# Attention over active tokens: values of later batches from the score stacks, and context products kept together

## The chip, the cores and the metric

The kernel runs on one core of one Trainium2 chip. The metric is device time in microseconds (us). The core has TensorE (PE, matrix products into PSUM), VectorE (DVE), ScalarE (ACT), GpSimd (POOL) and SyncE (SP), each with its own queue, worked off in order. TensorE's weight loads are listed apart, as PEld. DMA transfers are issued from SyncE's queue and, for rows picked by an index, from GpSimd's.

## The reference

There are 16 batches; x is 16 x 512 x 1024 (features x tokens). The queries serve as keys and as values too.

```python
xt = transpose(x, (0, 2, 1))                         # tokens x 512
q = xt @ Wq.T;  qh = q in 8 heads of 64
scores = 0.125 * einsum('bhqd,bhkd->bhqk', qh, qh)
logits = (scores * cmask + (1 - cmask) * -1e30) * rmask
ctx = einsum('bhqk,bhkd->bhqd', softmax(logits), qh)
x = x + transpose(ctx @ Wo.T)
```

The mask is 0 or 1 for each token. A masked key gets no weight. For a masked query all logits are equal, and its context is the mean of q over all tokens.

## The kernel before, in words

**Tokens.** Of each batch only the active tokens, at most C = 544, go through attention. An index is built on the chip from the mask (`active`, `slots`, `hot`, `index`), and `gather` fetches rows of x by it: four blocks of 128 slots and a tail of 32 (CT). Inactive tokens only get the projected mean added (`rest`).

**Stages of a batch n.** `xt` transposes a block on TensorE and splits it into two float16 parts, xh and xl. `query(n, e, g)` makes q for a pair of heads e (128 features) and half g of the slots, in 12 products. `qsplit(n, e)` then splits q of the pair into hi and lo float16 parts (`hl`), and four DMAs of SyncE spread them into the *score stack* xx. Its slices 0 and 2 hold, for the two heads of the pair, hi in partitions 0 to 63 and lo in partitions 64 to 127; slices 1 and 3 hold the same with hi and lo exchanged. The DMAs are not issued at once: `later` puts them off to the next step. There are five buffers for stacks, and a batch has four.

`value(n, e)` (L484) turns q of a pair into values, slots in the partitions, by four float32 transposes (L489), copies them to `v` on ScalarE (L491) and sums their squares for the softmax's shift (`peaks`, `top`, `bottom`: the largest norm of a head bounds its scores; group 0 is heads 0 to 3, group 1 heads 4 to 7). Six buffers hold `v`. `value_tail` does the same for the tail slots.

`scores(b, p, i)` makes four products of the stack (L611, 128 keys x 544 queries in two halves), and ScalarE takes their exponential (L615) into a tile of p. `scores(b, p, None)` does the tail keys of four heads (L586). `attend(b, p, i)` adds the context of one block of keys for a pair of heads to `pav`: four float32 products, two halves by two heads (L629). Each of them appears as two matmuls in the profile, "passes" below. Block 4 is the tail (L632). `recip_sums` and `recip_rows` make the reciprocals of the sums, `norm` multiplies them in, and `project` multiplies by Wo (L712) and adds to x; rows leave by an indirect DMA. `project_means` projects the means of a group of batches.

**What sets the order.** `run` goes through the batches. Batch b has 18 steps: for four pairs of heads p the blocks i = 0 to 3, and two tail steps. A step makes the scores of one head, then works off a share of a list m of other work, then makes the scores of the second head. The list m holds the projection of batch b - 1, the second shift group of b, and the transposes, queries, values and first shift group of batch n = b + 1, each item with a cost in us; `fill` takes from it in proportion. The contexts of two steps are put off and then called together, as a *context group*:

```python
if i in (0, 2):
    ready, todo = todo, []
elif i in (1, 3):
    for f in ready[1::-1] + ready[2:]:
        f()
    ready = []
```

Two attends make 8 float32 products, 16 passes. The order in which the instructions come to stand in an engine's queue is then settled by the framework's scheduler, which weighs priorities and its own estimates of when an operand is ready; so other work may come between two products of a group. `behind(i)` keeps what is recorded under it after instruction i, and `high_priority` lets it go ahead of other work that is ready.

Tiles of PSUM: two buffers for scores, one for `pav`, two (`pm`) for everything else.

Of the kernel before, what the change touches and what calls it, by code (L numbers as in the profile page):

```python
# [12 lines left out]
F16 = mybir.dt.float16  # L13
I32 = mybir.dt.int32
AF = mybir.ActivationFunctionType
ALU = mybir.AluOpType
# [3 lines left out]
P = 128  # L20
# [3 lines left out]
DK = 64  # L24
# [8 lines left out]
CH = C // 2  # L33
# [13 lines left out]
HPO = 300  # L47


class Fast:  # L50
# [12 lines left out]
    def __init__(self, ctx, tc, x, x_nat, mask_t, wq_t, wo_t, out):  # L63
        self.tc, self.nc = tc, tc.nc
        self.x, self.x_nat, self.out = x, x_nat, out
        self.B = x.shape[0] // T
        pool = lambda name, bufs, **k: ctx.enter_context(tc.tile_pool(name=name, bufs=bufs, **k))
        self.const = pool("const", 1)
        self.one = pool("one", 1)
        self.dram = pool("dram", 8, space=bass.MemoryType.DRAM)  # L70
        self.ps_s = pool("ps_s", 2, space=PS)
        self.ps_av = pool("ps_av", 1, space=PS)
        self.ps_m = pool("ps_m", 2, space=PS)
        self.st = {}
        self.scatters = []
        self.exp, self.pool = [], []

        self.paced, self.beat = False, None
        self.urgent, self.spare = [], []

        self.soon = []
        self.w, self.raw = {}, {}
        self.src = {"q": wq_t, "o": wo_t}
        self.setup(mask_t)
# [44 lines left out]
    def setup2(self):  # L129
        nc, fixed = self.nc, self.fixed  # L130

        self.quad = fixed("quad", [P, HG])
        nc.vector.tensor_reduce(self.quad, self.ident.rearrange("p (r t) -> p r t", r=HG), AX.X, ALU.add)
        self.xh = fixed("xh", [P, DC, CQ], F16)
        self.xl = fixed("xl", [P, DC, CQ], F16)
        for t in (self.xh, self.xl):
            nc.gpsimd.memset(t[:, :, CM + 1:], 0.0)

        self.rcol = [fixed("rcol%d" % k, [P, P]) for k in range(2)]
        self.smcol = [fixed("smcol%d" % k, [P, P]) for k in range(2)]  # L140
        for t in self.rcol + self.smcol:
            nc.gpsimd.memset(t, 0.0)

        self.big = fixed("big", [P, self.B + 2 * DC])

        self.par = fixed("par", [P, 2])
        nc.vector.tensor_tensor(self.par, self.quad[:, 0:2], self.quad[:, 2:4], ALU.add)
# [335 lines left out]
    def value(self, b, e):  # L483
        nc, s = self.nc, self.st[b]  # L484
        if e == 0:
            s["sd"] = self.sb([P, DC, H], F32, "sd")
        pv = self.pm([P, 4, P])
        for k in range(4):
            nc.tensor.transpose(pv[:, k, :], s["q"][:, e, k * P:(k + 1) * P], self.ident)  # L489
        v = self.sb([P, 4, P], F32, "v", 6)  # L490
        nc.scalar.copy(v, pv)  # L491
        s["v"].append(v)
        self.squares(v.rearrange("p k (h d) -> p (k h) d", h=2), s["sd"][:, e, :], e < 2 if b == 0 else e == 0, b == 0)
# [126 lines left out]
    def attend(self, b, p, i, ps):  # L620
        nc, s = self.nc, self.st[b]

        if i == 1:
            s["pav"] = self.ps_av.tile([P, 2, 512], F32, tag="av", name="pav")
        for g in range(2):
            for k in (1, 0) if i < 4 else range(2):
                cols = slice(g * CH, (g + 1) * CH)
                if i < 4:
                    nc.tensor.matmul(s["pav"][k * DK:(k + 1) * DK, g, :CH], lhsT=s["v"][p][:, i, k * DK:(k + 1) * DK],  # L629
                                     rhs=ps[k][:, cols], start=(i == 1), stop=False)  # L630
                else:
                    nc.tensor.matmul(s["pav"][:, g, :CH], lhsT=s["vt"][p // 2][:, k, p % 2 * 2:p % 2 * 2 + 2, :],  # L632
                                     rhs=s["pt"][:, p % 2, cols], start=False, stop=(k == 1))
        if i == 4:
            c = self.sb([P, C], F32, "c", 4)
            nc.scalar.copy(c.rearrange("p (g c) -> p g c", g=2), s["pav"][:, :, :CH])
            s["c"].append(c)
# [192 lines left out]
    def run(self, flag):  # L830
        B = self.B
        L = lambda f, *a: lambda: f(*a)
# [5 lines left out]
        def xt(n):  # L838
            return [(0.45, L(self.xt, n, c)) for c in range(4)] + [(0.25, L(self.xt, n, 4))]

        def query(n, e, g):
            u = [(1.37, L(self.query, n, e, g))]
            return u + [(0, L(self.qsplit, n, e))] if g else u

        def value(n, e):
            return [(0.45, L(self.value, n, e))]
# [8 lines left out]
        for i, e in enumerate(ends):  # L855
            g = list(range(ends[i - 1] + 1 if i else 0, e + 1))
# [73 lines left out]
        if True:  # L930
            for b in range(B + 1):
                o, n = b - 1, b + 1
# [3 lines left out]
                free, sums, rows, third, tail, rest = {}, [], [], [], [], []  # L936
                if b:
                    sums, rows, third = [(0, L(self.recip_sums, o, 3))], [(0.1, L(self.recip_rows, o, 3))], [(0, L(self.norm, o, 3))]
                if n < B:
                    if b in tails:  # L940
                        free[0] = [L(self.late, o, 4)]
                        tail = [(2.6, L(self.project_tail, o))]
# [3 lines left out]
                second = [(0, L(self.norm, o, 2))] if b else []  # L946
                P_ = (lambda *i: project(o, *i)) if b else (lambda *i: [])
                pk, tp, bt = ((lambda o, g, f=f, c=c: [(c, L(f, o, g))]) for f, c in ((self.peaks, 0), (self.top, 0.1), (self.bottom, 0.1)))
                new = [g for g in groups if b == g[0] - 2], [g for g in groups if b == g[0] - 1]
                if n < B:  # L950
                    q, x, v = (lambda e, g: query(n, e, g)), xt(n)[2 if b == 0 else 0:], (lambda e: value(n, e))
                    tc, tv = ((lambda g, f=f, c=c: [(c, L(f, n, g))]) for f, c in ((self.tail_copy, 0), (self.value_tail, 0.25)))
                    rng = [(0, L(self.range_x, n, c)) for c in range(DC)]
                    ahead = b + 2 < B
                    hot, index = ([(c, L(f, b + 2))] if ahead else [] for f, c in ((self.hot, 0), (self.index, 0.2)))
                    take = [(0, L(self.gather, b + 2, j)) for j in range(5)] if ahead else []
                    m = sums + pk(b, 1) + x[:2] + second + x[2:4] + rows + x[4:]
                    for g in new[0]:
                        m += [(0, L(self.active, *g))]
                    m += q(0, 0) + tp(b, 1) + q(0, 1)  # L960
                    for g in new[0]:
                        m += [(0.3, L(self.slots, *g))]
                    for g in new[1]:
                        m += [(0, L(self.facts_sums, *g))]
                    m += bt(b, 1) + q(1, 0) + v(0) + third + q(1, 1)
                    for g in new[1]:
                        m += [(0.1, L(self.facts_end, *g))]
                    m += tc(0) + rng[:2] + tail + v(1) + P_(0) + tv(0) + rest + P_(1) + hot + rng[2:] + q(2, 0) + index
                    m += pk(n, 0) + q(2, 1) + tp(n, 0) + P_(2) + take + v(2) + q(3, 0) + bt(n, 0)
                    m += q(3, 1) + tc(1) + [(0, L(self.means, n))] + P_(3) + v(3) + tv(1)  # L970
                    if b == 0:
                        k = next(k for k, (c, f) in enumerate(m) if f is index[0][1])
                        for c in range(DC):
                            m.insert(k + 1 + 3 * c, (0, L(self.split, "o", c)))
                else:

                    places = [("xi", 8), ("xa", 13)]
                    come = [[L(self.late, x, j, *places[k % 2]) for j in range(5, 9)] for k, x in enumerate(rests[b])]
                    leave = [[L(self.rest, x, j) for j in range(5, 9)] for x in rests[b]]
                    free[0] = [L(self.late, b, 4)] + come[0]  # L980
                    for c, l in zip(come[1:] + [[]], leave):
                        free[0] += c + l
                    m = second + sums + pk(b, 1) + [(2.6, L(self.project_means, b))] + rows + [(0.6, lambda: None)]
                    m += tp(b, 1) + [(0.6, lambda: None)] + bt(b, 1) + [(1.2, lambda: None)] + third + [(1.2, lambda: None)] + P_(0, 1, 2, 3)
                if b == 1:
                    m += [(0, L(self.range_w, "o", c)) for c in range(DC)]
                if b == B - 1:
# [1 line left out]
                if b == 0:  # L989
                    m = begin + m  # L990
# [22 lines left out]
                for st, (p, i) in enumerate(S):  # L1013
# [16 lines left out]
                    if i in (0, 2):  # L1030
                        ready, todo = todo, []
                    elif i in (1, 3):
                        for f in ready[1::-1] + ready[2:]:
                            f()
                        ready = []
# [158 lines left out]
```

## Time and profile before

| | |
|---|---|
| median of 3 runs | 1074.26 us (1073.34 to 1080.06) |
| profiled execution | 1082.2 us, span 1080.5 us |
| TensorE busy | 1053.5 us, 98% of the span |
| VectorE, ScalarE, GpSimd busy | 739.3, 679.0, 317.5 us |
| TensorE clock granted | 0.993 of full speed over the span |

In the page's groups a row names the line, the engine, the operation, the tiles written and read, their shapes and the count; then come busy time and the mean length of one in ns, and after the second bar the engine's idle time just before these instructions, with what ended most of it. Matmuls overlap: [...]the next starts long before it ends. In the timeline a line is a run of equal instructions: start, length, engine, line and count. The difference of two starts is what a run takes of TensorE's time. The lines quoted are of line numbers before the change; in the changed kernel 489 becomes 497, 629 becomes 643 and 586 becomes 595.

### The profile page before, as it was taken

Reading aid. Unit: us, or ns where it says so; the run is one execution under the profiler, and the core shown is the slowest. Engines: PE = TensorE matmul, PEld = TensorE weight load, DVE = VectorE, ACT = ScalarE, POOL = GpSimd, SP = SyncE. Lnnn points to the kernel's source line nnn. Section 1 sums busy time; section 2 is a strip of 40 time slices with the busy share of each in tenths; the row PEclk is TensorE's granted clock in tenths of the full one; section 3 lists DMA queues with packets and bytes.
Section 4 is the critical chain, followed back from the end, with each engine's and each line's share of the span. In section 5 each row is a group of like instructions: output and inputs, shape, how many; then the busy total and the mean of one; then the engine's idle time right before and its main releaser. Section 6 shows DMA issues by size and latency. Waiting matters only on the chain.

```text
span 1080.5 us, 23254 instructions
## 1 busy us (share of the span) xinstructions
PE 1053.5 (98%) x8386; PEld 698.3 (65%) x8386; DVE 739.3 (68%) x2375; ACT 679.0 (63%) x1722; POOL 317.5 (29%) x303
## 2 busy tenths in 40 slices
PE   7899999999999999999999999999999999999996
PEld 6566666666666666666666666666666676666553
DVE  5698668676765767767685676958577676757553
ACT  4786667566666756657666666766667565655550
POOL 2101022232401222332322323223232322234643
PEclk8999999999999999999999999999999999999999
DMA  5756565546655654666556566554765555466652
GB/s 186 218 152 167 138 175 157 170 139 191 173 141 156 170 168 145 189 192 172 175 143 194 168 182 188 154 172 134 211 190 171 179 149 154 134 179 195 193 165 85
DMA packets 78122, 181.35 MB, mean 168 GB/s; under 512 B 15008, under 2 KB 16800, under 8 KB 78000
## 3 DMA queue, kind: packets, MB, share of 16 engines
q1 hardware_dynamic: 56816, 111.62, 37.1%
q0 software_dynamic: 21184, 68.18, 19.8%
q8 instruction: 68, 1.11, 0.4%
q14 instruction: 54, 0.44, 0.1%
HBM read 92.34 MB, written 33.91 MB: 117 GB/s over the span
## 4 chain that ended last, share of the span: by engine, by line
PE 88%; DVE 5%; ACT 3%; issue 2%; DMA 1%; POOL 0%; another core or an unknown queue 0%; POOLq 0%; SPq 0%; ACTq 0%; DVEq 0%
PE pav L629 23%; PE pss L611 21%; PE pm L443 15%; PE pm L712 14%; PE pm L420 3%; PE pav L632 3%; PE pm L489 2%; PE pss L586 2%; PE pm L665 1%; ACT p L615 1%; PE pm L511 1%; ACT xm L365 1%; PE warm L303 1%; ACT p L590 1%; DVE p L596 1%
## 5 line engine op out<-in xcount | busy, mean ns | idle before, releaser
L615 ACT ACTIVATE p<-pss,nm 128x544 f32<-128x544 f32 x512 | 365.9, 717 | 231.8 <-PE pss L611 221.8
L611 PE MATMUL pss<-xx 128*128 128x272 f16 x2048 | 314.1, 280 | 3.2 <-ACT p L615 2.3
L629 PE MATMUL pav<-p,v 128*64 128x272 f32 x2048 | 273.5, 401 | 0.0
L611 PEld LDWEIGHTS <-xx 128*128 128x128 f16 x2048 | 193.1, 100 | 77.8 <-issue 31.3
L629 PEld LDWEIGHTS pav<-p,v 128*64 128x64 f32 x2048 | 131.9, 136 | 94.4 <-issue 34.0
L796 POOL DMA_INDIRECT y_out<-xa,idx x68 | 68.7, 1011 | 283.2 <-PE pss L611 83.9
L443 PE MATMUL pm<-xh,wqh 128*128 128x274 f16 (+1 forms) x512 | 143.7, 281 | 3.1 <-DVE xa L717 2.2
L443 PE MATMUL pm<-xh,wql 128*128 128x274 f16 (+1 forms) x512 | 143.2, 280 | 0.0
L443 PE MATMUL pm<-xl,wqh 128*128 128x274 f16 (+1 forms) x512 | 143.1, 280 | 0.0
L335 POOL DMA_INDIRECT xa<-x_in,idx x68 | 76.4, 1124 | 174.6 <-PE pss L611 64.4
L443 PEld LDWEIGHTS <-wqh 128*128 128x128 f16 x1024 | 99.1, 99 | 26.0 <-issue 7.1
L796 POOL DMA_INDIRECT y_out<-xi,idx x60 | 76.8, 1280 | 121.9 <-PE pss L611 43.3
L615 ACT ACTIVATION_READ_ACCUMULATOR p<-pss,nm 128x1 f32 x512 | 103.5, 202 | 0.0
L717 DVE SCALAR_TENSOR_TENSOR xa<-pm,xa 128x512 f32<-128x512 f32 x60 | 41.4, 690 | 87.7 <-PE pm L712 83.6
L335 POOL DMA_INDIRECT xi<-x_in,idx x60 | 62.1, 1036 | 109.8 <-PE pss L611 39.0
L712 PE MATMUL pm<-woh,ch 128*128 128x512 f16 x240 | 91.1, 379 | 0.0
L712 PE MATMUL pm<-woh,cl 128*128 128x512 f16 x240 | 91.0, 379 | 0.0
L712 PE MATMUL pm<-wol,ch 128*128 128x512 f16 x240 | 91.0, 379 | 0.0
L446 ACT ACTIVATE q<-pm 128x272 f32<-128x272 f32 (+1 forms) x128 | 50.6, 395 | 60.0 <-PE pm L443 52.5
L712 PEld LDWEIGHTS <-ch 128*128 128x128 f16 x480 | 46.4, 98 | 45.7 <-issue 1.3
L365 ACT ACTIVATE xm<-xm 128x1024 f32<-128x1024 f32 (+1 forms) x62 | 62.5, 1009 | 1.9 <-DMA xm<-x_nat_in 1.9
L783 DVE TENSOR_TENSOR xi<-xi,ub 128x512 f32<-128x512 f32 (+1 forms) x60 | 41.3, 691 | 30.5 <-PE pss L611 28.5
(191 smaller groups left out, 1562.5 us busy)
## 6 DMA issues: line engine op xcount, KB each, us to landing
xx<-hl SPq DMA_DIRECT2D x256, 136.0 KB
xm<-x_nat_in SPq DMA_DIRECT2D x56, 512.0 KB
rb<-rd SPq DMA_DIRECT2D x128, 136.0 KB
pt<-c SPq DMA_DIRECT2D x64, 136.0 KB
pt<-p SPq DMA_DIRECT2D x64, 136.0 KB
ub<-ud SPq DMA_DIRECT2D x16, 256.0 KB
xi<-x_nat_in SPq DMA_DIRECT2D x8, 256.0 KB
xa<-x_in,idx POOLq DMA_INDIRECT x68
```

What stands on the lines that cost most here:

```text
L335: dma = self.nc.gpsimd.indirect_dma_start(out=tile[:n], out_offset=None, in_=self.x, in_offset=bass.IndirectOffsetOnAxis(ap=idx, axis=0))
L365: self.nc.scalar.activation(s["xm"][k], s["xm"][k], AF.Copy, accum_out=s["ms2"][:, k:k + 1])
L420: self.pe = nc.tensor.transpose(pt[:, c, :], x[:n, c * P:(c + 1) * P], self.ident[:n, :n]).ins
L443: self.beat = nc.tensor.matmul(pq, lhsT=w[:, c, e * P:(e + 1) * P], rhs=xx[:, c, cols], start=(k == 0), stop=(k == 3 * DC - 1)).ins
L446: nc.scalar.activation(s["q"][:, e, cols], pq, AF.Copy, scale=1.0 / (SX * SW))
L611: self.beat = nc.tensor.matmul(pt[:, g, :CH], lhsT=xx[:, 2 * k, i * P:(i + 1) * P], rhs=xx[:, 2 * k + a, g * CH:(g + 1) * CH], start=(a == ...
L615: self.exp = [nc.scalar.activation(t.rearrange("p (g c) -> p g c", g=2), pt[:, :, :CH], AF.Exp, bias=s["nm"][p // HG][:, p % HG:p % HG + 1 ...
L629: nc.tensor.matmul(s["pav"][k * DK:(k + 1) * DK, g, :CH], lhsT=s["v"][p][:, i, k * DK:(k + 1) * DK], rhs=ps[k][:, cols], start=(i == 1), s ...
L712: nc.tensor.matmul(po[:cols.stop - cols.start], lhsT=a[:, e, cols], rhs=w[:, e, :], start=(e == 0 and k == 0), stop=(e == DC - 1 and k == 2))
L717: self.nc.vector.scalar_tensor_tensor(x, po, 1.0 / (SX * SW), x, ALU.mult, ALU.add)
L783: self.once(self.nc.vector.tensor_tensor(x[:n], x[:n], s["ub"][:n], ALU.add), self.beat)
L796: dma = self.nc.gpsimd.indirect_dma_start(out=self.out, out_offset=bass.IndirectOffsetOnAxis(ap=idx, axis=0), in_=x, in_offset=None)
```

## The change

Values of batches 1 to 15 are made of the score stack. A slice of it, 128 slots wide, is the stationary operand, and the moving one is `two`, a 128 x 64 float16 tile made of two identities one above the other. The product adds hi and lo of a head and puts slots into the partitions. A pair of heads takes 4 blocks x 2 heads = 8 products, in place of 4 transposes. Batch 0 keeps the transposes.

```diff
+        self.two = fixed("two", [P, DK], F16)
+        nc.vector.tensor_tensor(self.two, self.ident[:, :DK], self.ident[:, DK:], ALU.add)
...
         for k in range(4):
-            nc.tensor.transpose(pv[:, k, :], s["q"][:, e, k * P:(k + 1) * P], self.ident)
+            if b == 0:
+                nc.tensor.transpose(pv[:, k, :], s["q"][:, e, k * P:(k + 1) * P], self.ident)
+            else:
+                for h in range(2):
+                    nc.tensor.matmul(pv[:, k, h * DK:(h + 1) * DK], lhsT=s["xx"][e][:, 2 * h, k * P:(k + 1) * P],
+                                     rhs=self.two, start=True, stop=True)
```

The first product of a context group is remembered, and the group's others are recorded behind it with a high priority. `run` clears the memory ahead of each group.

```diff
                 if i < 4:
-                    nc.tensor.matmul(s["pav"][k * DK:(k + 1) * DK, g, :CH], lhsT=s["v"][p][:, i, k * DK:(k + 1) * DK],
-                                     rhs=ps[k][:, cols], start=(i == 1), stop=False)
+                    with ExitStack() as st:
+                        if self.group_first:
+
+                            st.enter_context(self.behind(self.group_first))
+                            st.enter_context(self.tc.high_priority(offset=HPO))
+                        mm = nc.tensor.matmul(s["pav"][k * DK:(k + 1) * DK, g, :CH], lhsT=s["v"][p][:, i, k * DK:(k + 1) * DK],
+                                              rhs=ps[k][:, cols], start=(i == 1), stop=False)
+                    self.group_first = self.group_first or mm.ins
...
                     elif i in (1, 3):
+                        self.group_first = None
```

A value now needs the stack's transfers, so the list m is put in another order. Values 0 to 2 of batch n stand further behind their queries. Value 3 goes into the next batch's list, ahead of the peaks of shift group 1. In batch 0 the index of batch 2 and its gathers come earlier. In the last batch the product of means comes later.

```diff
-                    m = sums + pk(b, 1) + x[:2] + second + x[2:4] + rows + x[4:]
+                    m = sums + x[:2] + (value(b, 3) if b else []) + pk(b, 1) + second + x[2:4] + rows + x[4:]
...
-                    m += q(0, 0) + tp(b, 1) + q(0, 1)
+                    m += q(0, 0) + tp(b, 1) + (q(0, 1) if b else bt(b, 1) + q(0, 1))
...
-                    m += bt(b, 1) + q(1, 0) + v(0) + third + q(1, 1)
+                    m += (bt(b, 1) if b else hot) + q(1, 0) + third + ([] if b else index) + q(1, 1) + ([] if b else take)
...
-                    m += tc(0) + rng[:2] + tail + v(1) + P_(0) + tv(0) + rest + P_(1) + hot + rng[2:] + q(2, 0) + index
-                    m += pk(n, 0) + q(2, 1) + tp(n, 0) + P_(2) + take + v(2) + q(3, 0) + bt(n, 0)
-                    m += q(3, 1) + tc(1) + [(0, L(self.means, n))] + P_(3) + v(3) + tv(1)
+                    m += rng[:2] + tc(0) + tail + v(0) + P_(0) + tv(0) + rest + v(1) + P_(1) + (hot if b else []) + rng[2:] + q(2, 0) + (index if b else [])
+                    m += pk(n, 0) + q(2, 1) + tp(n, 0) + P_(2) + (take if b else []) + q(3, 0) + v(2) + bt(n, 0)
+                    m += q(3, 1) + tc(1) + [(0, L(self.means, n))] + P_(3) + tv(1)
...
-                    m = second + sums + pk(b, 1) + [(2.6, L(self.project_means, b))] + rows + [(0.6, lambda: None)]
-                    m += tp(b, 1) + [(0.6, lambda: None)] + bt(b, 1) + [(1.2, lambda: None)] + third + [(1.2, lambda: None)] + P_(0, 1, 2, 3)
+                    m = second + sums + value(b, 3) + pk(b, 1) + rows + [(0.6, lambda: None)]
+                    m += tp(b, 1) + [(0.6, lambda: None)] + bt(b, 1) + [(2.6, L(self.project_means, b))] + third + [(1.2, lambda: None)] + P_(0, 1, 2, 3)
```

Values 0 to 2 also get a smaller cost in m, 0.25 in place of 0.45.

More of the change, by code (lines that the diff above doesn't have):

```diff
@@ L950, in run @@
                 if n < B:
-                    q, x, v = (lambda e, g: query(n, e, g)), xt(n)[2 if b == 0 else 0:], (lambda e: value(n, e))
+                    q, x, v = (lambda e, g: query(n, e, g)), xt(n)[2 if b == 0 else 0:], (lambda e: [(0.25, L(self.value, n, e))])
                     tc, tv = ((lambda g, f=f, c=c: [(c, L(f, n, g))]) for f, c in ((self.tail_copy, 0), (self.value_tail, 0.25)))
@@ L1032, in run @@
                     elif i in (1, 3):
+                        self.group_first = None
                         for f in ready[1::-1] + ready[2:]:
```

## The prediction

> **What bounds the kernel now.** I read the page's busy table first, then what TensorE waits for, then the spacing of its instructions in the timeline. The page:
>
> ```profile
> PE 1053.5 (98%) x8386; PEld 698.3 (65%) x8386; DVE 739.3 (68%) x2375; ACT 679.0 (63%) x1722; POOL 317.5 (29%) x303
> PE 88%; DVE 5%; ACT 3%; issue 2%; DMA 1%; POOL 0%; another core or an unknown queue 0%; POOLq 0%; SPq 0%; ACTq 0%; DVEq 0%
> L615 ACT ACTIVATE p<-pss,nm 128x544 f32<-128x544 f32 x512 | 365.9, 717 | 231.8 <-PE pss L611 221.8
> L629 PE MATMUL pav<-p,v 128*64 128x272 f32 x2048 | 273.5, 401 | 0.0
> ```
>
> TensorE is busy 98% of the span and holds 88% of the chain; ScalarE's exponentials sit idle 231.8 us before their starts, nearly all for score products. So TensorE's queue is the kernel: what leaves it shortens the span, what waits in it lengthens it. Busy time can't price that (matmuls overlap), so I use the step from one start to the next. These are three stretches of TensorE's timeline (start, length, line, operation, count):
>
> ```profile
> 225.19 0.63 PE L611 MATMUL pss<-xx 128*128 128x272 f16 x4
> 225.75 2.05 PE L629 MATMUL pav<-p,v 128*64 128x272 f32 x16
> 227.74 0.64 PE L611 MATMUL pss<-xx 128*128 128x272 f16 x4
> 228.21 1.04 PE L420 MATMUL pm<-ident,xa 128*128 128x128 f32 x8
> ...
> 230.10 0.68 PE L629 MATMUL pav<-p,v 128*64 128x272 f32 x4
> 230.71 1.09 PE L420 MATMUL pm<-ident,xa 128*128 128x128 f32 x8
> ...
> 304.80 0.60 PE L489 MATMUL pm<-ident,q 128*128 128x128 f32 x4
> 305.23 0.63 PE L611 MATMUL pss<-xx 128*128 128x272 f16 x4
> ...
> 263.40 0.35 PE L268 MATMUL pm<-oht,tmp 128*128 128x9 f16 x8
> 263.61 0.62 PE L611 MATMUL pss<-xx 128*128 128x272 f16 x4
> ```
>
> A value (four float32 transposes) takes 305.23 - 304.80 = 0.43 us, 109 ns each. A run of 16 context passes (a float32 product is two) takes 1.99 us, a run of 4 takes 0.61: 0.115 us a pass and 0.15 us a run. Four scores ahead of a run take 0.56 us, otherwise 0.47: 0.09 more for going in. Eight float16 products with 128-column stationaries of their own, nine columns wide, take 0.21 us.
>
> Summing the usual step of each pair of neighbours over the whole queue gives 1026 us, and the trace has 1068 between first and last matmul. Of the 42 us of idling, 15 lie in the first 60 us and 4 in the last 60; in between it is 1 to 2 us per 60 us. The middle has no slack, and work taken from it counts in full.
>
> **Values as products.** 60 of the 64 values (batch 0 keeps transposes) become eight float16 products 64 columns wide, each with its own 128x128 stationary from the score stack. The nearest rows are the 9-column products above (about 26 ns a step) and the warm-up products, 128 columns wide, 58 ns:
>
> ```profile
> 8.14 3.70 PE L303 MATMUL warm<-on 128*128 128x128 f16 x60
> ```
>
> A width of 64 lies between: I take 29 ns, so 8 x 29 = 0.23 us for 0.436, and 60 x 0.204 = **12.2 us off**; the bounds are 26 ns (-13.7) and 58 ns (+1.7). One rule speaks against this: the Trainium skill, "TensorE: Matmul & The Clock Gate", section "LDWEIGHTS (loading the stationary operand)", gives a load its columns over 1.2 GHz, 107 ns for 128. If loads followed one another at that pace, a value would cost 0.85 us and the edit 60 x 0.42 = 25 us more. This trace does show each such load lasting 96 to 100 ns, but the eight of line 268 started 26 ns apart: a load's length is not its step. I take the row.
>
> **The wait that goes, and the one that comes.** The transposes read q, fresh from ScalarE and VectorE:
>
> ```profile
>   DVE q L449: 5.6, 15
>   issue: 2.0, 9
>   ACT q L446: 1.6, 5
>   DVE idx L270: 0.6, 2
> ```
>
> (idle time before line 489: us, times.) Some 8 of these 9.8 us belong to the batches that change and go. Instead the first two weight loads of a value wait for the stack's four transfers: copy of q, three VectorE steps, four issues on SyncE, landing. In the packets of the trace the last one lands 5.5 to 9.4 us after the query product that starts it (mostly 6.5 to 7.5; fourth stack 6 to 9.4; batch 1 5.7 to 8.4). In the changed program I price the queue between that query product and the value with the same steps. Batches 2 to 15: at least 6.1 and mostly 7.1 or more for the first value (often with only one product there, the seven others 0.9 to 1.1 us later), 7.9 for the second, 8.1 to 8.6 for the third, 8 to 11.8 for the fourth, which had to go into the next batch since a fifth buffer frees late. So most are covered with 0 to 2 us to spare, and I put 0.1 us on each: 5 to 6 us. In batch 1 three distances are 4.3 to 6.1 us, short by 1 to 3 each: 4 us. Everything on TensorE stands behind such a wait, scores first, and ScalarE's exponentials behind them. Bounds for all of it: nothing, and 0.5 us for each of 56 plus 8, 36 us.
>
> **Context groups.** The trace has 174 runs of line 629: 99 of 16 passes, 46 of 4, 19 of 8, the others between. The changed queue has 128, 126 of them whole. 46 runs fewer x (0.15 + 0.09) = **11.2 us off**. Scores that stood inside a group come up to 1.4 us later; ScalarE's 231.8 us of idling covers it mostly, and without that cover the next scores would wait for their buffer. In one place of each batch three score groups now follow closely, the third starting 0.75 us after the last start of the first; product plus exponential take 0.28 + 0.72 = 1.0, so 0.25 us x 14 = +3.5. A query product comes close to its buffer's release in the same way: +1.
>
> **What else moves in TensorE's queue.** The 16 tail-score products of line 586 run four at a time (0.58 us in one run). In 14 batches they are now cut into 1, 12 and 3 by a reciprocal's transpose and two of x. Steps in the trace are 4 ns inside a four, 106 to the next four, 210 out: 0.21 + 0.56 + 0.22 = 0.99 us, **5.8 us on**. Other neighbours change by -2.4.
>
> **Moves I cost at nothing.** Value 3 takes its ScalarE copy and VectorE sum of squares into the next batch with it, and shift group 1 follows; its result is needed by step 9 of 18, and it is queued around step 4. If not, scores of head 4 would stop TensorE. Batch 0's index and its five gathers on POOL's queue come earlier; later queue entries are other gathers, and the core's DMA engines are 56 to 61% busy. The last batch's product of means goes behind the shift: 2.6 us that are due anyway, with its one row store and the broadcasts on SyncE; the last adds wait for them with most of the batch to go. The added identity is one VectorE operation in setup. Without cover each is worth 1 to 2 us, once.
>
> **Sum.** Off: 12.2 + 8 + 11.2 + 2.4 = 33.8. On: 5.8 + 5.5 + 4 + 4.5 = 19.8. Net -14; with the stack waits at nothing -23.5. Since the distances mostly exceed the landings I take -18. The profiled execution was 1082.2 us for a span of 1080.5, 8 us over the runs' median of 1074.26; -18 makes it 1064, and the median **1056**.
>
> **Rivals.**
> 1. *The stack wait takes the gain.* For: the distances exceed the landings by only a microsecond, and the shorter queue brings values nearer. Against: SyncE issues stacks 2 to 4 us after the query product, as before. At 0.3 us more per value, 17 us more: 1073, no change. It decides from about 0.2.
> 2. *The weight loads pace the products* (the slower side). If a value's loads pass at their 98 ns, eight take 0.78 us: 60 x 0.35 = 21 us on instead of 12.2 off, so 1056 + 33 = 1089. Values alone break even at 0.436/8 = 54 ns a product; the whole -18 is used up 18/480 = 38 ns above the 29, at 67 ns. For: every load row shows about 98 ns. Against: line 268 and the warm-up.
> 3. *All covered*: no stack wait, and scores late but hidden by ScalarE: -28, 1046.
> 4. *The grouping isn't felt*: what stood between passes costs its entry elsewhere. 11.2 us less gain, 1067. Against: 0.15 is paid on leaving line 629 whatever follows.
>
> **Chances.** My sum 0.57 (1050 to 1062), all covered 0.16, rival 1 0.13, rival 4 0.07, loads or a wait that I don't see 0.07. A change under 1% (10.7 us) can't be told from none here. Faster by over 1% means below 1063.5: my sum and rival 3 nearly whole, 0.75; within 1%: 0.17; slower: 0.08. The range reaches from full cover to rival 4: 1044 to 1068.
>
> **What the changed profile would show.** Line 497: 480 products, 29 ns apart (eight in 0.23 us). Line 643: 2048 passes in about 128 runs, 16 in 1.99 us. Weight loads of line 497 idle for "DMA xx<-hl" 5 to 10 us in total, most of it before 110 us. A batch in the middle 1.2 us shorter. Line 595 in three pieces. I am wrong if products step at 60 ns or more, if that DMA wait passes 20 us, or if scores wait for ScalarE by more than 10 us.

## The result, and the profile after

The changed kernel takes 1081.41 us (median of 6 runs, 1079.65 to 1084.29), the kernel before 1077.62 (median of 6). The ratio is 1.0039, with a 95% interval of 1.0023 to 1.0056: slower by 0.4%, where I had forecast 1056. The page of the changed kernel:

```profile
PE 1038.1 (96%) x8626; PEld 690.9 (64%) x8626; DVE 745.6 (69%) x2376; ACT 681.6 (63%) x1722; POOL 303.0 (28%) x303
PE 82%; DMA 7%; DVE 3%; ACT 2%; issue 2%; SPq 2%; POOL 0%; POOLq 0%; ACTq 0%; DVEq 0%
PE pav L643 21%; PE pss L620 19%; PE pm L727 15%; PE pm L447 14%; DMA xx<-hl 6%; PE pm L424 3%; PE pav L647 3%; PE pss L595 2%; PE pm L497 2%; PE pm L680 1%; ACT q L450 1%; SPq L470 1%; ACT p L624 1%; PE pm L520 1%; DMA rb<-rd 1%
```

TensorE's busy time fell by 15.4 us, and its part of the chain from 88% to 82%. What it gave up, the stack transfers took: "DMA xx<-hl" is 6% of the chain now. The steps of the new products and of the grouped passes are those that were forecast. From TensorE's timeline:

```profile
317.81 0.40 PE L497 MATMUL pm<-two,xx 128*128 128x64 f16 x8
318.04 0.63 PE L620 MATMUL pss<-xx 128*128 128x272 f16 x4
...
305.83 2.05 PE L643 MATMUL pav<-p,v 128*64 128x272 f32 x16
307.81 0.64 PE L620 MATMUL pss<-xx 128*128 128x272 f16 x4
```

Eight products take 0.23 us, 16 passes 1.98. But the first value of a batch often does not find its stack. This is batch 14's, with the wait in brackets:

```profile
888.85 0.63 PE L620 MATMUL pss<-xx 128*128 128x272 f16 x4
891.39 0.19 PE L497 MATMUL pm<-two,xx 128*128 128x64 f16 x1 [1.91 <-DMA xx<-hl]
891.41 0.62 PE L620 MATMUL pss<-xx 128*128 128x272 f16 x4
891.88 0.38 PE L727 MATMUL pm<-woh,ch 128*128 128x512 f16 x1
892.09 0.38 PE L727 MATMUL pm<-wol,ch 128*128 128x512 f16 x1
893.62 0.36 PE L497 MATMUL pm<-two,xx 128*128 128x64 f16 x7 [1.15 <-DMA xx<-hl]
```

TensorE stands still twice, for the first half of the stack and for the second.

To say where all of it went, I split TensorE's time between its first and last matmul in two. *Idle* is what a step exceeds the usual one of its pair of neighbours by, where that is over 60 ns. *Steps* is the rest. (The prediction's 42 us of idling counted smaller excesses too.) The last column is the idle time directly ahead of value products.

| kernel | steps, us | idle, us | ahead of value products |
|---|---|---|---|
| before | 1044.6 | 23.8 | - |
| changed | 1022.3 | 44.8 | 16.5 |
| e_nowait | 1023.3 | 29.4 | 2.2 |
| e_norest | 1023.7 | 31.2 | 5.0 |
| f_v0 | 1023.0 | 34.1 | 5.6 |
| f_b1 | 1021.8 | 28.7 | 4.3 |
| f_v0_tail | 1015.2 | 40.5 | 6.2 |
| e_values | 1042.7 | 31.2 | 13.2 |
| e_transp | 1036.0 | 34.2 | - |
| e_group | 1037.9 | 34.5 | - |
| e_group14 | 1038.4 | 24.0 | - |

The change took 22.3 us of steps away and put 21.0 us of idling in their place. The sum of a row is read off the trace; the line between its two numbers depends on what is called usual, and other choices put the growth of idling between 16 and 25 us. In the changed kernel's row the last column stays between 15 and 17. Each row is one execution: that of before ran 4.6 us over its kernel's median, so the first two rows differ by 1.3 us in favour of the changed kernel and the medians by 3.8 against it.

### The profile page after: what moved, and what is told of

Read it like the earlier page. It is cut to its first block, busy times and chain, and to the rows that moved or that the text cites. A ratio compares the mean times of both kernels' runs of the same rounds, so it can differ in the third digit from the quotient of the medians.

```text
span 1079.7 us, 23837 instructions
## 1 busy us (share of the span) xinstructions
PE 1038.1 (96%) x8626; PEld 690.9 (64%) x8626; DVE 745.6 (69%) x2376; ACT 681.6 (63%) x1722; POOL 303.0 (28%) x303
## 3 DMA queue, kind: packets, MB, share of 16 engines
q8 instruction: 70, 1.15, 0.5%
## 4 chain that ended last, share of the span: by engine, by line
PE 82%; DMA 7%; DVE 3%; ACT 2%; issue 2%; SPq 2%; POOL 0%; POOLq 0%; ACTq 0%; DVEq 0%
PE pav L643 21%; PE pss L620 19%; PE pm L727 15%; PE pm L447 14%; DMA xx<-hl 6%; PE pm L424 3%; PE pav L647 3%; PE pss L595 2%; PE pm L497 2%; PE pm L680 1%; ACT q L450 1%; SPq L470 1%; ACT p L624 1%; PE pm L520 1%; DMA rb<-rd 1%
## 5 line engine op out<-in xcount | busy, mean ns | idle before, releaser
L620 PE MATMUL pss<-xx 128*128 128x272 f16 x2048 | 317.6, 280 | 3.1 <-ACT p L624 2.7
L643 PE MATMUL pav<-p,v 128*64 128x272 f32 x2048 | 262.9, 399 | 0.0
L643 PEld LDWEIGHTS pav<-p,v 128*64 128x64 f32 x2048 | 135.6, 136 | 94.3 <-issue 27.1
L339 POOL DMA_INDIRECT xa<-x_in,idx x68 | 69.5, 1023 | 167.1 <-PE pss L620 71.0
L811 POOL DMA_INDIRECT y_out<-xi,idx x60 | 74.0, 1233 | 137.7 <-DVE xi L798 38.3
L711 DVE TENSOR_TENSOR c<-c,rb 128x544 f32<-128x544 f32 x64 | 46.1, 720 | 22.4 <-PE pss L620 11.1
```

The source lines that it names most:

```text
L339: dma = self.nc.gpsimd.indirect_dma_start(out=tile[:n], out_offset=None, in_=self.x, in_offset=bass.IndirectOffsetOnAxis(ap=idx, axis=0))
L620: self.beat = nc.tensor.matmul(pt[:, g, :CH], lhsT=xx[:, 2 * k, i * P:(i + 1) * P], rhs=xx[:, 2 * k + a, g * CH:(g + 1) * CH], start=(a == ...
L643: mm = nc.tensor.matmul(s["pav"][k * DK:(k + 1) * DK, g, :CH], lhsT=s["v"][p][:, i, k * DK:(k + 1) * DK], rhs=ps[k][:, cols], start=(i == ...
L711: self.once(nc.vector.tensor_tensor(c, c, s["rb"][p], ALU.mult), self.beat if p < 3 else None)
L811: dma = self.nc.gpsimd.indirect_dma_start(out=self.out, out_offset=bass.IndirectOffsetOnAxis(ap=idx, axis=0), in_=x, in_offset=None)
```

## The experiments

The theory after the first look was that the landing of the stacks ate the gain. The rival was that TensorE would idle anyway, for buffers of scores and queries, since a shorter queue only runs into ScalarE and VectorE sooner.

**The same products without the wait.** Values 0 to 2 of batches 1 to 15 read a stack that has long landed, that of another pair:

```diff
-lhsT=s["xx"][e][:, 2 * h, k * P:(k + 1) * P],
+lhsT=(s["xx"][e] if e == 3 else self.st[b - 1]["xx"][3])[:, 2 * h, k * P:(k + 1) * P],
```

> The changed kernel, but values 0 to 2 of batches 1 to 15 read the stack of pair 3 of the batch before, which landed long ago: the same products, in the same places, without a wait for the landing. (The values are then those of other heads; this is left out of the result's meaning.) In the changed kernel's trace the value products idle 16.5 us beyond their usual steps. Theory (the landing waits took the gain): about 16 us under the changed kernel, 1063 to 1068 us, ratio to the kernel before 0.986 to 0.991. Rival (the gain was lost in idling elsewhere, at score and query buffers, and would be lost there again): within 4 us of the changed kernel, ratio 1.000 to 1.006.

Measured: 1066.41 us, ratio 0.9897 (0.9873 to 0.9922). The steps are those of the changed kernel, the idling ahead of the products fell from 16.5 to 2.2 us, and the time by 15. The view of what TensorE's multiplies waited for, first line of the changed kernel:

```profile
PE pm L497 <- DMA xx<-hl: 11.4, 15, 1.9
```

There is no such line for this kernel, and its weight loads of line 497 waited for a landing once:

```profile
PEld L497 <- DMA xx<-hl: 1.5, 1, 1.5
```

The landing waits cost 15 us, and nothing took their place. That part of the rival is out.

**Undoing one part at a time.** First transposes for all values, with the new order of m and the grouping kept:

```diff
-            if b == 0:
+            if True:
                 nc.tensor.transpose(pv[:, k, :], s["q"][:, e, k * P:(k + 1) * P], self.ident)
```

> The changed kernel with transposes for the values of all batches; its grouping of context products and its order of the list m are kept. The usual steps of its queue sum to 1023.7 us, against 1028.7 before and 1008.1 changed. Theory: no landing waits, transposes back at 12 us: 4 to 6 us under the kernel before, ratio 0.993 to 0.998, so faster than the changed kernel although its queue holds more work. Rival (grouping or the order is what costs): ratio 1.002 or more.

Measured: 1083.85 us, ratio 1.0057 (1.0040 to 1.0074); the changed kernel, with products in the same order, is 2.4 us faster. My theory missed here. No value waits for a stack, and steps are 8.6 us fewer than before, yet it is no faster. In its profile the reciprocals' transposes wait for VectorE, in nine places by 0.7 to 0.9 us over the usual step. TensorE's weight loads show it (us in total, times, longest):

```profile
PEld pm L680 <- DVE nm L560: 9.1, 9, 1.0
```

The changed kernel has no such wait. These waits are 8 of the 10 us by which the kernel with transposes idles more than the one before. Why VectorE is late there only with transposes was not followed further.

Then the grouping alone, on the kernel before (the diff is the change's own in `attend` and `run`), and the changed kernel without it:

```diff
-                        if self.group_first:
+                        if False:
```

> The kernel before with the grouping of context products alone. 128 runs of context passes in place of 174, but tail scores cut into 61 runs in place of 34. Sum of usual steps 5 us less than before. Theory: ratio 0.993 to 0.998. Rival (a group kept whole delays scores and the gain comes back as idling before scores): ratio 0.999 to 1.005.

> The changed kernel without the grouping: products for values and the new order of m alone. The queue has 204 runs of context passes, its usual steps sum to 1027.2 us, 1.5 less than before. Theory: the landing waits of some 16 us come on top, less about 4 us of waits of the old values: ratio 1.006 to 1.013. Rival (values as products gain their 12 us and grouping is what loses them): ratio 0.990 to 0.998.

Measured: grouping alone 1083.38 us, ratio 1.0054 (1.0035 to 1.0072); values and order alone 1092.52, ratio 1.0143 (1.0126 to 1.0160). The second is what the theory says, a little beyond its end, and it shows that in the new order the grouping is worth 11 us: 1092.5 against 1081.4. Without it context passes come in 204 runs. The first looks like a contradiction: on the old order grouping costs 6 us, with 6.7 us fewer steps. TensorE's timeline of grouping alone, in the last batch:

```profile
1020.71 0.39 PE L612 MATMUL pss<-xx 128*128 128x272 f16 x2
1025.90 0.48 PE L672 MATMUL pm<-ident,rcol 128*128 128x128 f32 x1 [4.79 <-DVE rcol L666]
1026.17 1.57 PE L612 MATMUL pss<-xx 128*128 128x272 f16 x6
1027.53 0.63 PE L719 MATMUL pm<-woh,ch 128*128 128x512 f16 x1
1027.95 0.63 PE L719 MATMUL pm<-wol,ch 128*128 128x512 f16 x1
```

Two of a head's four score products stand ahead of a reciprocal's transpose, which waits 4.79 us for VectorE. So I took the last batch out of the grouping:

```diff
-self.group_first = self.group_first or mm.ins
+self.group_first = (self.group_first or mm.ins) if b < self.B - 1 else None
```

> The kernel before with the grouping of context products in all batches but the last. In the trace of e_group the last batch's reciprocal waits 5.0 us for VectorE at 1025.9 us, which the kernel before does not show. Theory (grouping loses in the last batch, and elsewhere breaks even): 4 to 6 us under e_group, ratio 0.998 to 1.001. Rival (grouping loses a little everywhere): ratio 1.003 or more.

Measured: 1077.26 us, ratio 0.9990 (0.9979 to 1.0001), 6 us less than with it. The loss of grouping alone lies in the last batch, where the trace shows that one wait and the half clock at it (last section). In the changed kernel's last batches (from 1020 us on) only 1.1 us of idling is left, so this is no part of its loss. But the other 15 batches gain nothing clear of noise either, 2 us at most, though the table counts 6.2 us fewer steps. On the old order grouping is thus hardly felt, on the new one it is worth 11 us; why is not shown.

**Why the stack is late.** SyncE issues the first stack mostly sooner than before, 2.1 us after its query product ends (before 2.6 to 3.0). But batch 14's four issues stand behind those of other transfers (SyncE's timeline):

```profile
880.03 0.46 SPq L611 DMA_DIRECT2D pt<-c  x1
880.59 1.20 SPq L688 DMA_DIRECT2D rb<-rd  x2
881.90 0.54 SPq L612 DMA_DIRECT2D pt<-p  x1
882.48 0.59 SPq L611 DMA_DIRECT2D pt<-c  x1
883.12 0.59 SPq L612 DMA_DIRECT2D pt<-p  x1
884.22 0.46 SPq L468 DMA_DIRECT2D xx<-hl  x1
884.72 0.60 SPq L469 DMA_DIRECT2D xx<-hl  x1
885.37 0.61 SPq L470 DMA_DIRECT2D xx<-hl  x1
886.86 0.46 SPq L471 DMA_DIRECT2D xx<-hl  x1
```

Three gathers of inactive rows fall into the same stretch. A table by stretch (busy time of PE, PEld, DVE, ACT and POOL, clock, share of the 16 DMA engines, GB/s) has the engines full:

```profile
883.00:895.00 12.00, 8.94 (x72) 5.70 (x71) 7.20 (x29) 7.43 (x20) 3.02 (x3) 0.96 1.00 234
```

The stack's last quarter, issued at 886.86, is there at 893.5. None of this is new: in the kernel before the last quarter of batch 14's first stack is issued at 887.49, completes at 894.6, and the engines are nearly as full (0.95):

```profile
887.49 1.32 SPq L467 DMA_DIRECT2D xx<-hl  x1
884.00:896.00 12.00, 11.97 (x91) 7.98 (x91) 9.43 (x31) 8.86 (x24) 3.33 (x4) 1.00 0.95 251
```

To test whether full engines make stacks late I left the gathers out, in both kernels (`rests` stays empty, so no inactive row is read, changed or written):

```diff
-                rests.setdefault(min(e + 1 + (k if e < B - 3 else k // 2), B - 1), []).append(b)
```

> The changed kernel without the inactive tokens' rows: they are neither gathered, nor given the projected mean, nor written (60 gathers, 60 adds and 60 scatters left out). The order of TensorE's queue stays as it is but for that. In the changed kernel the DMA engines were full from 883 to 895 us, by four transfers of the tail's exponentials, two of the reciprocals, three gathers of such rows and the first stack. Theory (contention made the first stack late): the wait of the value products for landings falls from 16.5 us to 4 to 8, and the ratio to the same kernel made from before (the next run) is 0.985 to 0.993. Rival (the landings are late by the issue on SyncE, not by full DMA engines): the wait stays over 13 us.

> The kernel before without the inactive tokens' rows, the yardstick of the run before it. TensorE's queue has no such work in it, so both theories expect 1072 to 1078 us, ratio 0.995 to 1.001.

Measured: the changed kernel 1064.90 us, ratio to the full kernel before 0.9892 (0.9853 to 0.9932); the kernel before 1075.96, ratio 0.9994 (0.9975 to 1.0013). The first over the second is 0.990. The idling ahead of value products fell from 16.5 to 5.0 us, that of first values from 11.0 to 0.3. The same stretch of batch 14 in the kernel without the gathers:

```profile
876.00:888.00 12.00, 12.00 (x99) 8.13 (x98) 9.46 (x33) 8.52 (x22) 0.00 (x0) 1.00 0.68 179
```

There the last quarter is issued at 880.36 and complete at 883.7, and the last seven products start after that without a wait:

```profile
880.36 0.60 SPq L471 DMA_DIRECT2D xx<-hl  x1
884.59 0.37 PE L497 MATMUL pm<-two,xx 128*128 128x64 f16 x7
```

Over batches 1 to 15 the last quarter of the first stack completes 2.4 to 6.6 us after its issue in the changed kernel (median 4.8), and 2.3 to 3.9 without the rows (median 2.4), while the issue follows the query product by 2.1 us in most batches of both. So the first stack was late on the DMA engines and not on SyncE. The edit takes the rows' gathers, writes and adds together; it doesn't tell which of these transfers did it. The kernel before gains nothing clear of noise by it (0.9975 to 1.0013): there no value hangs on a stack.

**Giving the stack time.** Value 0 moves behind the first projected block and value 1 behind the second:

```diff
-tail + v(0) + P_(0) + tv(0) + rest + v(1) + P_(1)
+tail + P_(0) + tv(0) + rest + v(0) + P_(1) + v(1)
```

> The changed kernel with values 0 and 1 moved further back in the list m: value 0 behind the first projected block and the rest's adds, value 1 behind the second. On TensorE's queue value 0 then stands 11 to 18 us behind the query product that its stack comes from, in place of 6 to 10, value 1 14 to 20 us in most batches. In the changed kernel value 0 waited 11.0 us and value 1 2.3 of 16.5 in all. Theory (a late first stack): the wait for landings falls to 3 to 5 us, time 1067 to 1071 us, ratio to before 0.990 to 0.995. Rival (transfers land late wherever the value stands, since the shorter queue only moves the wait): ratio 0.999 or more.

Measured: 1070.03 us, ratio 0.9934 (0.9919 to 0.9949). First values waited 1.1 us in place of 11.0, second ones nothing; 3.5 us are left at third values. The wait does not follow the value: the rival is out here too, and the kernel is 11 us faster than the changed one.

The tail scores, cut into three pieces by the change's order, were then kept together on top of that, in the manner of a context group:

```diff
+                            if a or g or r:
+                                st.enter_context(self.behind(tails_first))
+                                st.enter_context(self.tc.high_priority(offset=HPO))
```

> As the run before it, and the 16 tail-score products are kept together like a context group: 34 runs of them in place of 61. By the usual steps of the queue 6.7 us less. Theory: 4 to 7 us under the run before it, ratio to before 0.984 to 0.991. Rival (a tail group kept whole makes the transposes of x and the reciprocals late, and gives it back): within 2 us of the run before it.

Measured: 1071.16 us, ratio 0.9956 (0.9936 to 0.9975). The 7.8 us of steps went, and the idling rose by 6.4, of which 4.8 ahead of scores. The rival's number was right, though not its reason, which was late transposes: keeping the tail scores together gained nothing in the end.

Last the start, on top of f_v0's order. Batch 1 keeps its transposes too, and batch 0's list m is the one before the change:

```diff
-            if b == 0:
+            if b < 2:
...
-(value(b, 3) if b else [])
+(value(b, 3) if b > 1 else [])
```

> As f_v0, but batch 1 keeps its transposes too, and batch 0's list m is that of the kernel before: index and gathers of batch 2 in their old place, no value of batch 1 on a stack. In the trace of f_v0 TensorE idles 20.1 us up to 120 us, in that of the kernel before 11.6; 1.3 us of work is added. Theory (the reordered start costs what batch 1 gains, and more): 4 to 7 us under f_v0, ratio to before 0.987 to 0.990. Rival (the idling at the start is set by the first loads and stays): within 2 us of f_v0, ratio 0.992 to 0.996.

Measured: 1065.84 us, ratio 0.9885 (0.9857 to 0.9913), 4 us under f_v0 by the medians and 0.5% by the ratios. Up to 120 us TensorE idles 14.0 us in place of 20.1. This version is 1.2% faster than the kernel before.

## Why the prediction was wrong

**What held.** Products at 29 ns a step: measured 29. Runs of passes: 174 to 128, the steps of passes 7.4 us fewer and those of scores 3.7, together 11.1 for 11.2 (46 x 0.24 is 11.0). Tail scores in pieces: 5.1 us for 5.8. All steps together: -22.3 for -20.0 (12.2, 11.2 and 2.4 off, 5.8 on). The weight loads do not pace the products; that rival is out. Rival 4, grouping that isn't felt, is out for the new order alone.

**What failed** is "The wait that goes, and the one that comes" (1 and 2) and "Moves I cost at nothing" (3).

1. *"the last one lands 5.5 to 9.4 us after the query product that starts it (mostly 6.5 to 7.5"*. This reading of the trace before is the step that failed. By the completion signals of the transfers, the first stacks of batches 1 to 15 land in that same trace 6.7 to 11.6 us after the end of the query product, with a median of 9.6, and nine of the 15 after more than 9.4. (Their data packets, read apart, give a median of 8.9.) In the changed kernel it is 6.3 to 11.3, median 9.3. So the change did not make them later; they had been late where no value waited for them. How the shorter figures came about is not on record. The distances were right: the first values that waited stand 7.2 to 9.2 us behind their query product, where I had "mostly 7.1 or more", and each waits for most of the time that is missing up to its landing. So *"I put 0.1 us on each"* and 4 us for batch 1, 9.5 us, became 16.5. Of these 11.0 are at first values, which I had thought covered, and only 2.3 in batch 1. I had looked at DMA only as a mean share of 56 to 61%. My own bound of 0.5 us for each value was in sight of this.
2. *"Some 8 of these 9.8 us ... go"*: 3.5 went (idling ahead of transposes 4.5 us before, 1.0 after). The view of a line adds up the idle times of the weight loads and of the multiplies, so it counts one wait twice. The changed kernel's view of line 497 shows it too: 23.5 us, where the waits by engine have 12.1 for loads and 11.4 for multiplies. My sign of being wrong, 20 us of that wait, was passed only in this double count.

```profile
  DMA xx<-hl: 23.5, 26
```

3. *"Moves I cost at nothing ... without cover each is worth 1 to 2 us, once"*: up to 120 us TensorE idled 18.0 us, against 11.6 before, and 2.3 of that are batch 1's stack waits, counted above. The last experiment gained 4 us by undoing batch 0's moves and batch 1's products together; which of the two it was is not separated.

These are 7.0, 4.5 and 4.1 us, about the 15 by which the idling (21.0 measured, 6 in my sum) was missed. Scores and queries idled 3.1 us more, where I had put 4.5; projections 2.3 us more, of which 1.7 are steps at half the clock (last section).

The rest of the 25 us between 1056 and 1081 lies outside these terms. The sum gave -14, and I took -18 because "the distances mostly exceed the landings", the same misreading: 4 us. The base was 3 us low, a median of 1074 from three runs where all six give 1077.6. And the profile from which I priced the change is of an execution 4.6 us over that median. From 960 us on it idles 5.2 us, where the kernel before without the gathers idles 1.5; so part of the idling that I started from need not be in the other runs.

Rival 1 named what happened: stack waits take the gain. I had given it 0.13. Its price, 17 us on top of the 9.5, was too high, since all waits of values came to 16.5, and its 1073 is still 8 us under the result.

## What to carry to other kernels

Where an operand made on the core is replaced by one that arrives by DMA, count the landing in the stretch where it falls, with the queue and the share of DMA engines there; a mean share over the kernel (58% here) hides stretches that are full (95 to 100%). Where nobody waits for a transfer, no wait tells that it is late: read each landing from its completion, transfer by transfer. Some other work put between issue and use was worth about as much here (11 us) as the cheaper instruction on paper (12 us). Steps from start to start price a full engine well; what they leave out is who else has to be on time.

## What the runs showed of the hardware that was not expected

A wait can cost more than its length. After the two waits of 1.91 and 1.15 us, TensorE was granted half its clock for 3.4 us:

```profile
889.00:894.00 5.00, 1.94 (x20) 1.04 (x18) 3.52 (x13) 2.42 (x6) 1.23 (x1) 1.00 1.00 252
894.00:897.40 3.40, 3.40 (x9) 1.21 (x8) 0.69 (x1) 1.22 (x2) 0.00 (x0) 0.50 0.73 166
898.00:902.00 4.00, 4.00 (x34) 2.68 (x32) 0.83 (x2) 2.80 (x7) 0.99 (x1) 1.00 0.26 33
```

Projections 512 wide then step by 0.43 us in place of 0.216, eight times over, which is 1.7 us lost on top of the 3.1:

```profile
894.46 0.63 PE L727 MATMUL pm<-wol,ch 128*128 128x512 f16 x1
894.89 0.63 PE L727 MATMUL pm<-woh,cl 128*128 128x512 f16 x1
```

In the grouping alone the clock was at half from 1025.7 to 1029.1 us, at the end of the wait of 4.79 us (its steps from 1027.53 to 1027.95). The Trainium skill, "TensorE: Matmul & The Clock Gate", section "Part 1: The HAM clock gate", has the clock fall after an idle window of some 3.4 us. Here 3.1 us of waits within 5 us, with a little work between them, were enough: in the 3.4 us ahead of the fall TensorE was busy for 1.47. In the run without waits for stacks a single wait of 1.88 us for VectorE was followed by the same:

```profile
683.30:686.60 3.30, 1.53 (x13) 0.86 (x10) 1.17 (x6) 1.13 (x4) 0.94 (x1) 1.00 1.04 224
686.70:690.00 3.30, 3.29 (x15) 2.16 (x15) 3.30 (x21) 0.59 (x2) 0.00 (x0) 0.50 1.05 278
```

And one wait of 3.26 us near the changed kernel's start was not; there the clock stayed full until 40.7 us:

```profile
14.92 0.63 PE L424 MATMUL pss<-ident,xa 128*128 128x128 f32 x4 [3.26 <-DMA xa<-x_in,idx]
```

So the length of a wait alone doesn't decide it. Outside its start and end the changed kernel shows the fall once.
